# A written order for the head of a macaron block: FFN weight, four norms and five FFNs

## The chip, the core and the metric

The kernel runs on one core of one Trainium2 chip. The metric is the device time of one execution in microseconds (us), the median of several. Five engines matter: TensorE (PE: matmuls and transposes, with its weight loads as PEld), VectorE (DVE), ScalarE (ACT), GpSimd (POOL), and SyncE (SP), which here only issues DMAs. Each engine works through its own queue in order and waits on semaphores for the others.

## The reference: what is computed

The input is x of 4 x 4096 rows with 512 channels. One block is applied:

```
x = x + 0.5 * ffn(layernorm(x))
x = x + attention(layernorm(x))      # 16 heads of 32, 13 neighbours of each row, relative bias
x = x + 0.5 * ffn(layernorm(x))      # the same weight
```

The FFN is one 512 x 512 product with a bias. Before it, both operands are quantised: each run of 32 values in a row of the activations and of the weight is divided by its scale (its largest magnitude / 7.5), rounded to the nearest value of a 6-bit grid, ties to the lower one, and multiplied by the scale again. The attention has a product for queries, keys and values (1536 x 512, with bias) and an output product (512 x 512, with bias).

## The kernel before: stages, slots and the names that matter

**Tiles.** The 16384 rows are 128 tiles of 128 rows (`t`); four tiles make a group. Every large product is made in f16 parts: each operand is a high half and a low half, and `product` (L146 to L155) makes 12 matmuls of 128x128 by 128x512 (three pairs of halves, four chunks of channels). All weights lie in `wt`, channels first, in columns `QO, KO, VO, PO, FO` for queries, keys, values, output product and FFN.

**Stages of a tile.** `load`; `moments` (mean and variance on DVE); `quantised_norms`: POOL makes the factors, ACT the normed rows `yq`, DVE the block scales `sc` and `r`, POOL multiplies (L246), ACT rounds to fp8, POOL multiplies back (L251), ACT and DVE make the two halves `hlq`, and a transposing DMA makes `xT`. Then `ffn` (PE into `pmf`, DVE adds into x, L279), `first_half` (the attention's norm, halves `hln`, transposing DMA into `x2`), `values` (PE into `pmv`, halves `vt`, to DRAM), `project_qk`, `softmax`, `attend` and `project_out` by items of a group and a quarter of the channels, and `second_half` (the second FFN).

**The order of the work.** `begin(slot, stage, rank)` puts a stage (a Python generator) into a slot; `run_slot` runs what lies in a slot by rank, and each `yield n, rank` moves the rest n slots on. A tile comes every `STEP` = 7 slots: its first FFN at slot 7t+5, its values at 7t+20, the first query and key product at slot 38 (`QK`). From `manual_schedule()` on, the program order is the order of each engine's queue; before that call, a planner with its own times reorders the instructions.

**The head.** Inside the `setup` pool and ahead of `manual_schedule()`, so ordered by the planner, stand: loads of the FFN weight `fw`, of three tiles of x and of the 16 chunks `rows` of the other weights; the sums of squares (ACT, `junk`), from which `powers` makes power-of-two scales `up` and `down`; the FFN weight's block scales (`w_abs`, `w_sc`, `w_hi`, `w_lo`, `w_r`, L730 to L743); its quantisation in four chunks (L757 to L774; the two products of `wu` at L760 and the one at L771 are POOL's); four transposing DMAs that put it into `wt` (`put_weights`); and the quantised norms of tiles 0 to 2. After `manual_schedule()`, `put_scaled` (L789, L791) scales and splits the 16 other chunks, in slots 2 to 36, each with a transposing DMA; `scales` (slot 0), `put_table` (slot 26) and `attention_bias` (slot 28, a product `pmb`) stand beside them.

Of the kernel before, what the change touches and what calls it, by code (L numbers as in the profile page):

```python
# [37 lines left out]
P = 128  # L38
# [26 lines left out]
def macaron_kernel(  # L65
# [70 lines left out]
    def tie_to_lower(t):  # L136

        nc.vector.scalar_tensor_tensor(t, t, BELOW_ONE, t, ALU.mult, ALU.min)
        ti = t.bitcast(I32)
        nc.vector.tensor_scalar(ti, ti, 1, None, ALU.bitwise_or)

# [74 lines left out]
    def quantised_norms(slot):  # L220

        tiles, mv = together.pop(slot)
        n = len(tiles)
        rs, nb = factors(slot, "q", mv[0], n)
# [21 lines left out]
        nc.gpsimd.tensor_tensor(yb, yb, bc(r, QB), ALU.mult)  # L246
# [4 lines left out]
        nc.gpsimd.tensor_tensor(  # L251
# [3 lines left out]
        if spare:  # L255
            hl = xp.tile([P, dim], F32, tag="x", name=f"hlq{slot}").bitcast(F16)
            hl = hl.rearrange("p (u s k) -> p u s k", u=1, s=2)
        else:
            hl = hlp.tile([P, 2, 2, dim], F16, tag="hlq", name=f"hlq{slot}")[:, :n]
# [11 lines left out]
    def ffn(t, which):  # L271

        xT = ys.pop(t)
        pm = ps_m.tile([P, dim], F32, tag="mm", name=f"pm{which}_{t}")
        product(
            pm, lambda s, c: xT[:, s, c, :], lambda s, c: wt[:, s, c, FO : FO + dim]
        )
        yield 1, 8
        nc.vector.scalar_tensor_tensor(xs[t], pm, cf, xs[t], ALU.mult, ALU.add)  # L279

    def first_half(t):

        yield from ffn(t, "f1")
        yield 1, 2
        mv = sm.tile([P, 1, 2], F32, tag="mvn2", name=f"mvn2_{t}")
        statistics(t, "n2", mv[:, 0, :])
        yield 1, 2
        rs, nb = factors(t, "n2", mv)
        yield 1, 2
        y = yp.tile([P, 1, dim], F32, tag="yn2", bufs=1, name=f"yn2_{t}")  # L290
        nc.scalar.activation(y[:, 0], xs[t], AF.Identity, bias=nb, scale=rs)
        hl = hlp.tile([P, 1, 2, dim], F16, tag="hln2", name=f"hln2_{t}")
# [274 lines left out]
    EARLY = 3  # L567
    STEP = 7

    F1, V, QK, SC, PV, OUT, F2 = 5, 2 * STEP + 6, 5 * STEP + 3, 6 * STEP, 8 * STEP + 3, 13 * STEP + 2, 12  # L570

# [32 lines left out]
    for t in range(NT):  # L604
        k = t * STEP
        begin(k - 18, one(load, t), 0)
        enlist(k - 10, t, "n1")
        if not 0 < t < EARLY:
            begin(k - 11, one(moments, k - 10, t, "n1"), 1)
        begin(k + F1, first_half(t))  # L610
        begin(k + V, values(t))
        begin(k + F1, one(add_bias, t, half_ffn_b), 8)
        at = out_slot(t)
        begin(at - 5, one(add_bias, t, after_b), 8)
        enlist(at + 2, t, "n3")
        begin(at, project_out(t, at + 2))
        begin(at + 6 if t < LAST else second_slot(t) - 2, one(add_bias, t, half_ffn_b), 8)
        begin(second_slot(t), second_half(t))
    for slot in together:
        if slot >= EARLY * STEP - 10:  # L620
            begin(slot, quantised_norms(slot), 1)
# [12 lines left out]
    with tc.tile_pool(name="setup", bufs=1) as sp, tc.tile_pool(name="scratch", bufs=2) as scr:  # L634
# [10 lines left out]


        rows = {}

        sq = sp.tile([P, 5 * KC], F32, name="sq")
        first = min(slots)  # L650
        for slot in range(first, first + EARLY * STEP, STEP):
            run_slot(slot)
        for _ in quantised_norms(-10):
            pass
        chunks = (8, 9, 10, 11, 12, 13, 14, 15, 0, 4, 1, 5, 2, 6, 3, 7)
        for o in chunks:
# [3 lines left out]
        for o in (*range(4 * KC, 5 * KC), *chunks):  # L660
            src = fw[:, o - 4 * KC, :] if o >= 4 * KC else rows[o]
            junk = scr.tile([P, dim], BF16, tag="junk", name=f"junk{o}")
            nc.scalar.activation(junk, src, AF.Square, accum_out=sq[:, o : o + 1])
        ptb = ps_m.tile([P, 512], F32, tag="mm", name="ptb")
        nc.tensor.transpose(ptb[:, : 3 * KC], b12, ident[: 3 * KC, : 3 * KC])
        bT = sp.tile([P, 3 * KC], F32, name="bT")
        nc.vector.tensor_copy(bT, ptb[:, : 3 * KC])
        b2 = sp.tile([P, 3 * KC], F32, name="b2")
        nc.vector.scalar_tensor_tensor(b2, bT, 2.0 ** -8, bT, ALU.mult, ALU.mult)
        nc.vector.tensor_tensor(sq[:, : 3 * KC], sq[:, : 3 * KC], b2, ALU.add)  # L670
        top5 = sp.tile([P, 5], F32, name="top5")
        up = sp.tile([P, 5], F32, name="up")
        down = sp.tile([P, 5], F32, name="down")

        def powers(lo, hi):
# [7 lines left out]
            nc.tensor.transpose(ptn[:w, :P], top5[:, lo:hi], ident)  # L683
            most = sp.tile([w, 1], F32, name=f"most{lo}")
            nc.vector.tensor_reduce(most, ptn[:w, :P], AX.X, ALU.max)
            diag = sp.tile([w, w], F32, name=f"diag{lo}")
            nc.vector.tensor_scalar(diag, ident[:w, :w], most, 2.0, ALU.mult, ALU.mult)
            ones_w = sp.tile([w, P], F32, name=f"ones{lo}")
            nc.gpsimd.memset(ones_w, 1.0)
            pb = ps_m.tile([P, 512], F32, tag="mm", name=f"pb{lo}")  # L690
            nc.tensor.matmul(pb[:, :w], ones_w, diag, start=True, stop=True)
            e = sp.tile([P, w], I32, name=f"e{lo}")
            nc.vector.tensor_copy(e.bitcast(F32), pb[:, :w])
            nc.vector.tensor_scalar(e, e, 23, None, ALU.logical_shift_right)
            nc.vector.tensor_scalar(e, e, 131, None, ALU.add)
            nc.vector.tensor_scalar(e, e, 1, None, ALU.logical_shift_right)
            nc.vector.tensor_scalar(e, e, 97, None, ALU.max)
            u, d = up[:, lo:hi].bitcast(I32), down[:, lo:hi].bitcast(I32)
            nc.vector.tensor_scalar(u, e, -1, 264, ALU.mult, ALU.add)
            nc.vector.tensor_scalar(u, u, 23, None, ALU.logical_shift_left)  # L700
            nc.vector.tensor_scalar(d, e, -10, None, ALU.add)
            nc.vector.tensor_scalar(d, d, 23, None, ALU.logical_shift_left)

        powers(4, 5)
        nc.vector.tensor_scalar(cf, down[:, 4:5], 0.5 / XS, None, ALU.mult)
        nc.gpsimd.tensor_scalar(half_ffn_b, half_ffn_b, 0.5, None, ALU.mult)
# [9 lines left out]
        def small(name):  # L716
            return sp.tile([P, KC * NB], F32, name=name)

        w_abs, w_sc, w_hi, w_lo, w_r = (
            small(s) for s in ("w_abs", "w_sc", "w_hi", "w_lo", "w_r")  # L720
        )

        def split_scale():
            nc.vector.tensor_scalar(
                w_hi.bitcast(I32), w_sc.bitcast(I32), -4096, None, ALU.bitwise_and
            )
            nc.vector.tensor_tensor(w_lo, w_sc, w_hi, ALU.subtract)

        for o in range(KC):
# [4 lines left out]
        nc.vector.tensor_scalar(w_sc, w_abs, 1.0 / Q_MAX, None, ALU.mult)  # L734
        split_scale()
        nc.vector.scalar_tensor_tensor(w_abs, w_hi, -Q_MAX, w_abs, ALU.mult, ALU.add)
        nc.vector.scalar_tensor_tensor(w_abs, w_lo, -Q_MAX, w_abs, ALU.mult, ALU.add)
        nc.vector.scalar_tensor_tensor(w_sc, w_abs, 1.0 / Q_MAX, w_sc, ALU.mult, ALU.add)
        nc.vector.tensor_scalar(w_sc, w_sc, Q_EPS, None, ALU.max)
        nc.vector.reciprocal(w_r, w_sc)  # L740
        split_scale()
        w_back = small("w_back")
        nc.vector.tensor_scalar(w_back, w_sc, up[:, 4:5], F8_SCALE, ALU.mult, ALU.mult)  # L743

        def large(name, o, dt=F32):
            return scr.tile(
                [P, NB, QB], dt, tag=name, bufs=3 if name == "wu_" else KC, name=f"{name}{o}"
            )

        for o in range(KC):  # L750
# [5 lines left out]
            qh, q0 = large("wqh_", o, F16), large("wq0_", o)  # L756
            nc.vector.tensor_tensor(qh, fwb, per(w_r), ALU.mult)  # L757
            for i, b in enumerate((w_hi, w_lo)):
                u = large("wu_", f"{o}_{i}")
                nc.gpsimd.tensor_tensor(u, qh, per(b), ALU.mult)  # L760
                nc.vector.tensor_tensor(fwb, fwb, u, ALU.subtract)  # L761
            nc.vector.tensor_tensor(q0, fwb, per(w_r), ALU.mult)
            nc.vector.tensor_tensor(q0, q0, qh, ALU.add)  # L763
            q0f = q0.rearrange("p n q -> p (n q)")
            tie_to_lower(q0f)
# [5 lines left out]
            nc.gpsimd.tensor_tensor(fwb, w8, per(w_back), ALU.mult)  # L771
            hl = scr.tile([P, 2, dim], F16, tag="whl", bufs=4, name=f"whlf{o}")
            nc.scalar.copy(hl[:, 0, :], fw[:, o, :])
            nc.vector.tensor_tensor(hl[:, 1, :], fw[:, o, :], hl[:, 0, :], ALU.subtract)  # L774
            put_weights(4 * KC + o, hl)

        for t in range(1, EARLY):
            moments(t * STEP - 10, t, "n1")
            for _ in quantised_norms(t * STEP - 10):
                pass  # L780

        ctx.enter_context(tc.manual_schedule())

        def put_scaled(o):
            s = up[:, o // KC : o // KC + 1]
            hl = scr.tile([P, 2, dim], F16, tag="whl", bufs=4, name=f"whl{o}")
            nc.scalar.activation(hl[:, 0, :], rows[o], AF.Copy, scale=s)  # L789
            yield 1, 9  # L790
            nc.vector.scalar_tensor_tensor(  # L791
# [132 lines left out]
```

## Time and profile before

| what | us |
|---|---|
| median of 3 runs (lowest, highest) | 2367.79 (2367.39, 2368.29) |
| the profiled execution's own time | 2366.79 |
| its span, first to last instruction | 2365.0 |
| PE busy, share of the span | 2273.6 (96%) |
| DVE busy | 2022.5 (86%) |
| POOL busy | 1987.6 (84%) |
| ACT busy | 1326.8 (56%) |
| first matmul of an FFN | 58.23 |
| first matmul of a query and key product | 105.73 |

The span is 1.8 us shorter than the execution's own time, and that execution is 1.0 us below the median. "Busy" is the time in which an engine has an instruction under way; a duration in the trace includes what an instruction waits for within the engine, so the same operation can show 0.6 us alone and 1.5 us beside another engine. Instructions on one engine overlap by a little: the start of the next one is a better price than a duration. A matmul group of one `product` is shown as x12.

### The profile page before, as it was taken

How to read it: one execution, taken by the hardware profiler on the slowest of the kernel's cores; microseconds unless marked ns; L12 is line 12 of the kernel's file. 1: busy time of each engine (PE TensorE's matmuls, PEld its weight loads, DVE VectorE, ACT ScalarE, POOL GpSimd, SP SyncE). 2: the span in 40 equal slices, each digit the busy share in tenths (PEclk: the TensorE clock that was granted, in tenths of full speed). 3: DMA queues.
4: the chain of work that ended last, by engine and by line, in shares of the span. 5: the costliest groups of instructions: out<-in, count | busy, mean ns of one | idle time of the engine just before them, and what ended most of it. 6: DMA issues, size and time to landing. Idle time of an engine off the chain costs nothing.

```text
span 2365.0 us, 82328 instructions
## 1 busy us (share of the span) xinstructions
PE 2273.6 (96%) x35539; PEld 1115.4 (47%) x35539; DVE 2022.5 (86%) x3588; ACT 1326.8 (56%) x2080; POOL 1987.6 (84%) x2012
## 2 busy tenths in 40 slices
PE   0799999999999999999999999999999999999988
PEld 0255444444444444444444444444444444444543
DVE  8799888888888888888888888888888888888785
ACT  4466556555555555555555565555555555555542
POOL 5588888888888888888888888888888888888886
PEclk9899999999999999999999999999999999999999
DMA  5789787787777777777777778777777778677763
GB/s 154 146 168 165 156 160 155 147 159 156 151 157 152 156 158 153 156 152 158 153 157 153 153 159 154 153 154 156 158 151 160 151 152 160 153 152 155 133 121 104
DMA packets 925701, 360.59 MB, mean 152 GB/s; under 512 B 718876, under 2 KB 889752, under 8 KB 925336
## 3 DMA queue, kind: packets, MB, share of 16 engines
q1 hardware_dynamic: 924992, 354.79, 73.3%
q8 instruction: 278, 4.55, 0.9%
q10 hardware_dynamic: 344, 0.53, 0.1%
q14 instruction: 87, 0.71, 0.1%
HBM read 110.15 MB, written 67.29 MB: 75 GB/s over the span
## 4 chain that ended last, share of the span: by engine, by line
PE 94%; DVE 3%; DMA 1%; POOL 1%; issue 1%; ACT 0%; SPq 0%; DVEq 0%; ACTq 0%; POOLq 0%
PE pmqk L151 28%; PE pmf L151 27%; PE pmo L151 14%; PE pmv L151 14%; PE ps L442 7%; PE pv L512 3%; DVE fw L761 0%; DMA xT<-hlq 0%; DMA fw<-in_L_ffn_weight_dram 0%; DVE stn L180 0%; DVE wq L763 0%; DVE hlq L204 0%; DVE wqh L757 0%; DMA rows<-in_L_attn_qkv_w_dram 0%; DVE whl L791 0%
## 5 line engine op out<-in xcount | busy, mean ns | idle before, releaser
L151 PE MATMUL pmf<-wt,xT 128*128 128x512 f16 x3048 | 703.5, 381 | 9.1 <-DMA xT<-hlq 9.1
L151 PE MATMUL pmqk<-x,wt 128*128 128x512 f16 x3072 | 705.7, 379 | 1.4 <-DVE vt L315 1.4
L151 PEld LDWEIGHTS <-xT 128*128 128x128 f16 x3048 | 299.1, 98 | 373.7 <-DMA xT<-hlq 11.5
L151 PEld LDWEIGHTS <-wt 128*128 128x128 f16 x3072 | 289.6, 98 | 336.6 <-issue 1.9
L151 PE MATMUL pmv<-wt,x 128*128 128x512 f16 x1536 | 355.0, 381 | 5.1 <-DVE mvn L181 5.1
L246 POOL TENSOR_TENSOR yq<-yq,r 128x1024 f32<-128x1024 f32 (+1 forms) x141 | 246.5, 1748 | 130.0 <-DVE r L244 130.0
L151 PE MATMUL pmo<-wt,ring 128*128 128x512 f16 x1536 | 354.8, 381 | 0.8 <-issue 0.8
L573 POOL TENSOR_TENSOR x<-x,half_ffn_b 128x512 f32<-128x512 f32 x256 | 327.4, 1279 | 0.1
L279 DVE SCALAR_TENSOR_TENSOR x<-pmf,coef,x 128x512 f32<-128x512 f32 x256 | 179.7, 702 | 156.4 <-PE pmf L151 155.9
L314 ACT CAST vt<-pmv 128x512 f16<-128x512 f32 x128 | 74.9, 585 | 388.9 <-PE pmv L151 388.9
L539 ACT ACTIVATE ring<-pv 128x510 f16<-128x510 f32 (+8 forms) x224 | 82.3, 414 | 368.4 <-PE pv L512 368.4
L180 DVE BATCH_NORM_STATS2 stn<-x 128x6 f32<-128x512 f32 x384 | 265.3, 691 | 8.9 <-DMA x<-in_L_attn_x_dram 0.2
L251 POOL TENSOR_TENSOR yq<-q,sc 128x1024 f32<-128x1024 fp8e4 (+1 forms) x141 | 246.7, 1749 | 0.0
L151 PEld LDWEIGHTS <-x 128*128 128x128 f16 x1536 | 150.8, 98 | 188.1 <-DMA x<-hln 5.6
L377 DVE SCALAR_TENSOR_TENSOR qk<-pmqk,qk_b,qk 128x512 f16<-128x512 f32 x256 | 190.5, 744 | 42.2 <-ACT qk L373 41.1
L151 PEld LDWEIGHTS <-ring 128*128 128x128 f16 x1536 | 140.7, 98 | 159.4 <-issue 3.3
L249 ACT ACTIVATE q<-yq,nudge 128x1024 fp8e4<-128x1024 f32 (+1 forms) x141 | 149.9, 1063 | 114.3 <-POOL yq L246 106.1
L485 POOL TENSOR_TENSOR sf<-sf,total 128x714 f32<-128x714 f32 (+2 forms) x128 | 178.6, 1395 | 34.5 <-ACT yq L233 19.1
L373 ACT ACTIVATE qk<-pmqk,qk_b 128x512 f16<-128x512 f32 x256 | 176.1, 688 | 52.1 <-PE pmqk L151 50.8
L186 POOL TENSOR_SCALAR rsq<-mv 128x2 f32<-128x2 f32 (+1 forms) x141 | 130.1, 923 | 89.3 <-DVE mv L181 86.6
L233 ACT ACTIVATE yq<-x,nbq,rsq 128x512 f32<-128x512 f32 x254 | 193.0, 804 | 18.0 <-POOL nbq L192 17.5
L492 POOL TENSOR_TENSOR p<-sf,p 128x714 f16<-128x714 f32 (+2 forms) x128 | 192.6, 1504 | 0.0
(145 smaller groups left out, 3459.7 us busy)
## 6 DMA issues: line engine op xcount, KB each, us to landing
vs<-vd SPq DMA_DIRECT2D x144, 357.0 KB
x<-in_L_attn_x_dram SPq DMA_DIRECT2D x128, 256.0 KB
vd<-vt SPq DMA_DIRECT2D x128, 256.0 KB
out_dram<-x SPq DMA_DIRECT2D x128, 256.0 KB
vs<-vd SPq DMA_DIRECT2D x24, 378.0 KB
vs<-vd SPq DMA_DIRECT2D x24, 315.0 KB
rows<-in_L_attn_qkv_w_dram SPq DMA_DIRECT2D x12, 256.0 KB
xT<-hlq SPq DMA_TRANSPOSE x141
```

Of the source, the lines that this page charges most:

```text
L151: nc.tensor.matmul(pm, lhs(a, c), rhs(b, c), start=(n == 0), stop=(n == 3 * KC - 1))
L180: nc.vector.bn_stats(st, xs[t])
L233: nc.scalar.activation(y[:, u], xs[t], AF.Identity, bias=nb[:, u : u + 1], scale=rs[:, u : u + 1])
L246: nc.gpsimd.tensor_tensor(yb, yb, bc(r, QB), ALU.mult)
L251: nc.gpsimd.tensor_tensor(yb, q8.rearrange("p u (n q) -> p (u n) q", q=QB), bc(sc, QB), ALU.mult)
L279: nc.vector.scalar_tensor_tensor(xs[t], pm, cf, xs[t], ALU.mult, ALU.add)
L373: nc.scalar.activation(t[:, s, 0, KN:], pms[s], AF.Identity, bias=bias)
L377: nc.vector.scalar_tensor_tensor(t[:, s, 1, KN:], pms[s], bias, t[:, s, 0, KN:], ALU.add, ALU.subtract)
L442: nc.tensor.matmul(ps[rows, u, :sides, w * KN : (w + 1) * KN], t[rows, 0, part, q0 : q0 + QR], t[rows, 1, :sides, k0 : k0 + KN], start=par ...
L485: nc.gpsimd.tensor_tensor(s, s, bc(total[:, :n], KN), ALU.mult)
L492: nc.gpsimd.tensor_tensor(p[:, :n, KN : 2 * KN], s, ph, ALU.subtract)
L573: nc.gpsimd.tensor_tensor(xs[t], xs[t], b, ALU.add)
```

## The change

All of the head is put under `manual_schedule()`, and its order is written out: generators for the small and the large steps are advanced one at a time by `run(generator, n)`, and `both(o, n)` takes one step each of the weight's chunks o and o+1 with a small step behind each.

- POOL's three products of each FFN weight chunk go to DVE. So do both products of the quantised norms of tiles 0 to 3 (`mult`).
- The FFN weight and the values' weight get their channels first by TensorE transposes into PSUM (16 and 16 of 128x128 f32), from which ACT and DVE write the halves into `wt`: 8 transposing DMAs fewer.
- The norms of tiles 0 to 3 are written between the weight's steps; tiles 4 and 5 follow. FFN 0 and 1 are begun with the first half of the output channels (`begin_ffn`), as soon as two chunks of the weight are there.
- The first five FFNs, the values' weight and the start of the values of tile 0 follow in the written order. The slot loop then starts at 23 instead of 0. FFN 5 stands at slot 31 (before: 40), values 1, 2 and 3 at 24, 27, 33 (before: 27, 34, 41).
- `put_scaled` is left with 12 chunks, at slots 23, 25, 33, 35 (queries and keys of the first two quarters), 42, 44, 49, 51 and, for the output product, 56, 60, 64, 67 (before: all 16 by slot 36). `attention_bias` goes from slot 28 to 70, `put_table` from 26 to 31.
- The loads of six tiles of x and of `rows` are issued at the head in one list; the bias of tiles 0 and 1 is added by DVE, the FFN bias is halved by ACT.

The core of the diff:

```diff
+        mult = nc.vector if slot in N1[:4] else nc.gpsimd
...
-        nc.gpsimd.tensor_tensor(yb, yb, bc(r, QB), ALU.mult)
+        mult.tensor_tensor(yb, yb, bc(r, QB), ALU.mult)
...
+    def begin_ffn(t):
+        xT, n = ys[t], dim // 2
+        pm = ps_m.tile([P, dim], F32, tag="mm", name=f"pmf1_{t}")
+        product(pm[:, :n], lambda s, c: xT[:, s, c, :], lambda s, c: wt[:, s, c, FO : FO + n])
+        begun[t] = pm, n
...
+    N1 = (-6, -5, -4, -3, -2, -1)
+    FIRST, VALUES = (5, 6, 11, 20, 23, 31), (18, 21, 27, 33)
+    SOON, AHEAD = len(FIRST), 5
...
+        ctx.enter_context(tc.manual_schedule())
+        def run(g, n=1):
+            for _ in range(n):
+                next(g, None)
...
+        def channels_first(pt, w):
+            for c in range(KC):
+                nc.tensor.transpose(pt[:, c, :], w[:, c * P : (c + 1) * P], ident)
+        def values_weight(o, pt):
+            channels_first(pt, rows[o])
+            yield
+            h, l = (wt[:, s, :, o * P : (o + 1) * P] for s in (0, 1))
+            s = up[:, o // KC : o // KC + 1]
+            nc.scalar.activation(h, pt, AF.Copy, scale=s)
+            yield
+            nc.vector.scalar_tensor_tensor(l, pt, s, h, ALU.mult, ALU.subtract)
+            yield
...
+            for b in (w_hi, w_lo):
+                nc.vector.tensor_tensor(u, qh, per(b), ALU.mult)
+                yield
                 nc.vector.tensor_tensor(fwb, fwb, u, ALU.subtract)
+                yield
...
-            nc.gpsimd.tensor_tensor(fwb, w8, per(w_back), ALU.mult)
-            hl = scr.tile([P, 2, dim], F16, tag="whl", bufs=4, name=f"whlf{o}")
...
+            nc.vector.tensor_tensor(fwb, w8, per(w_back), ALU.mult)
...
+            channels_first(pt, fw[:, o, :])
+            h, l = (wt[:, s, :, FO + o * P : FO + (o + 1) * P] for s in (0, 1))
+            nc.scalar.copy(h, pt)
+            yield
+            nc.vector.tensor_tensor(l, pt, h, ALU.subtract)
+            yield
...
+        def both(o, n=1):
+            for _ in range(n):
+                run(ready[o])
+                run(small_ones)
+                run(ready[o + 1])
+                run(small_ones)
...
+        both(2)
+        begin_ffn(0)
+        moments(n1_slot(2), 2, "n1")
+        run(norms[2])
+        run(norms[1])
+        squares(*chunks[11:14])
+        both(2)
+        run(norms[2])
+        run(norms[1])
+        begin_ffn(1)
...
+        small_ones = powers(0, 4)
+        run(small_ones)
+        moments(n1_slot(3), 3, "n1")
+        run(norms[3])
+        run(ready[2])
+        run(ready[3])
+        run(norms[3])
+        run(small_ones)
+        run(norms[2], 2)
...
+        both(2)
+        firsts = {t: first_half(t) for t in range(AHEAD)}
+        run(firsts[0])
+        run(firsts[1])
+        run(v_weight[11])
+        run(norms[2])
+        run(norms[3])
...
-        for slot, o in zip((2, 4, 5, 6, 10, 13, 16, 19, 21, 23, 25, 27, 29, 31, 33, 35), chunks):
+        begin(24, one(scales), 3)
+        begin(24, firsts[3], 4)
+        begin(24, first_values[1], 5)
+        begin(24, norms[5], 1)
+        begin(26, firsts[4], 1)
+        for slot, o in zip((23, 25, 33, 35, 42, 44, 49, 51, 56, 60, 64, 67), chunks[4:]):
             begin(slot, put_scaled(o), 9)
-        begin(28, attention_bias(), 9)
-        begin(26, one(put_table), 9)
-        slot = first
+        begin(70, attention_bias(), 9)
+        begin(31, one(put_table), 9)
+        slot = min(slots)
```

## The prediction, made before the changed kernel ran

> **What bounds the kernel now.** I read the page's engine and slice rows first, then a table of busy time by stretch, then the timeline of PE, then that of DVE and POOL in the head.
>
> ```profile
> PE 2273.6 (96%) x35539; PEld 1115.4 (47%) x35539; DVE 2022.5 (86%) x3588; ACT 1326.8 (56%) x2080; POOL 1987.6 (84%) x2012
> PE   0799999999999999999999999999999999999988
> ```
>
> PE is full from the fourth slice on. Its idle time lies in the first two slices and at the end. The change doesn't touch the end, so only the head can pay. The table by stretch (columns: PE, PEld, DVE, ACT, POOL busy; PE clock; DMA share; GB/s) says who holds the head up:
>
> ```profile
> 7.00:20.00 13.00, 1.04 (x4) 0.58 (x4) 12.25 (x36) 9.96 (x29) 7.83 (x13) 1.00 0.98 356
> 20.00:35.00 15.00, 0.00 (x0) 0.00 (x0) 15.00 (x22) 4.25 (x13) 12.17 (x10) 1.00 0.24 72
> 35.00:47.00 12.00, 0.93 (x3) 0.58 (x3) 12.00 (x23) 4.85 (x8) 5.29 (x3) 1.00 0.26 50
> 47.00:58.20 11.20, 0.00 (x0) 0.00 (x1) 9.28 (x23) 5.78 (x9) 4.39 (x4) 1.00 0.52 100
> 72.90:82.50 9.60, 5.31 (x13) 1.67 (x13) 7.12 (x12) 5.82 (x10) 6.23 (x9) 0.68 0.67 137
> 94.00:105.70 11.70, 8.92 (x32) 3.48 (x32) 10.94 (x20) 6.63 (x11) 7.08 (x11) 0.78 0.88 168
> 105.70:117.30 11.60, 11.57 (x176) 5.72 (x176) 7.20 (x14) 5.63 (x9) 7.39 (x11) 1.00 0.64 139
> 128.90:140.50 11.60, 11.60 (x191) 5.72 (x177) 10.94 (x24) 7.62 (x13) 9.93 (x13) 1.00 1.06 210
> 140.50:152.80 12.30, 12.30 (x256) 6.21 (x243) 11.40 (x25) 7.86 (x14) 10.11 (x13) 1.00 0.88 161
> ```
>
> Until 58 us DVE is the bound; from 58 to 105.7 nobody is full: PE waits for chains through DVE, POOL, ACT and a DMA; from 105.7 PE is. Note the last two rows: there DVE has only 0.7 to 0.9 us idle in seven slots. PE's timeline shows what is done by then:
>
> ```profile
> 58.23 4.41 PE L151 MATMUL pmf<-wt,xT-10_160 128*128 128x512 f16 x12 [15.20 <-DMA wt<-whlf]
> 62.47 2.75 PE L151 MATMUL pmf<-wt,xT-3_391 128*128 128x512 f16 x12
> 82.49 4.24 PE L151 MATMUL pmf<-wt,xT 128*128 128x512 f16 x12 [4.27 <-DMA xT<-hlq]
> 105.73 5.34 PE L151 MATMUL pmqk<-x,wt 128*128 128x512 f16 x24 [1.40 <-DVE vt L315]
> ```
>
> By 105.73 PE has made five FFNs, three value products and `pmb`: nine, at 2.6 us from start to start when warm, 23 us of 106.
>
> **DVE and POOL in the head.** Price of a 128x512 step on DVE:
>
> ```profile
> 24.65 0.62 DVE L761 TENSOR_TENSOR fw<-fw,wu 128x512 f32<-128x512 f32 x1
> 26.64 1.53 DVE L761 TENSOR_TENSOR fw<-fw,wu 128x512 f32<-128x512 f32 x1
> 29.05 1.49 POOL L760 TENSOR_TENSOR wu<-wqh,w_hi 128x512 f32<-128x512 f16 x1
> 48.12 1.02 DVE L696 TENSOR_SCALAR e<-e 128x4 int32<-128x4 int32 x1
> ```
>
> The same step starts the next after 0.60 us alone and 1.46 us beside a POOL product; even a step of four elements took 1.02. Going through DVE's timeline from 14.9 to 52.1 us, some 20 instructions are stretched, by 15.5 us in all (start-to-start minus 0.60, or minus 0.12 for a small one). The change puts 20 products of POOL's on DVE in this stretch (12 of the weight, 8 of norms): 20 x 0.60 = 12.0. Here a rule speaks against it: the Trainium skill, "Perfetto Trace Analysis", section "Optimizing Scalar/DVE Operations", says that when DVE is saturated, moving work off to Scalar or even GpSimd may make sense, though the shared read port may spoil it. DVE is saturated here, so by the offloading half this move loses 12.0 us; by the rows it wins 15.5 - 12.0 = 3.5. I take the rows, since they show both cases of the same instruction.
>
> **Stage 1, to the complete FFN weight.** From 7.1 (second chunk landed) DVE has in the written order: three maxima 1.8; four chunks of ten steps at 0.60 and one at 0.36, 25.4; norms 0 and 1 whole at 3.7 (statistics 0.82, scales 1.09, two products, low half), 7.4; norm 2 without its low half 3.1; norm 3 up to its first product 2.5; some 50 small steps at 0.12, 6.1. Sum 46.3, so 53.4. Waits that I see: `powers(0, 4)` has its transpose on PE behind the begun FFN 1, which waits for `xT` of tile 1. The price of that way is the row at 77.43, where a low half ending at 79.19 let PE start at 82.49: 3.3 us, then 12 cold half-width matmuls of about 2.2 and a transpose of 0.37; DVE stands 3 us for it, with norms 2 and 3 and both last weight chunks queued behind. About 1.5 for the last PE transposes (four at the 0.37 of `ptn`, then ACT 0.6) and the hops of `powers(4, 5)`. So 58: no earlier than the 58.2 of now. The eight DMAs saved (3.3 us from issue to landing) lie in this sum as shorter hops. At the bounds: no waits 54, each doubled 62.
>
> **Stage 2, to the end of the written list.** Now only FFNs and halves are left, since norms 0 to 3 are made. DVE: four `first_half` additions with statistics at 1.48 (5.9), four values' weights at 0.66 (2.6), two bias additions (1.2), norm 4's scales (1.1), eight products and low halves at 0.60 (4.8), two statistics at 0.82 (1.6), small ones 0.6: 17.9. Beside it POOL makes four products (norm 4, two biases); each stretches at most one step by 0.86, so 0 to 3.4, I take 2.0; and about 1.3 for `vt` behind a cold value product. 58 + 21.2 = 79.2.
>
> **Stage 3, slots 24 to 38.** Up to norm 5's low half at slot 29 DVE has its scales 1.1, `scales` 0.8, two scaled chunks 1.3, two `vt` 1.2, an addition with statistics 1.5, two low halves 1.2: 7.1, and 8.1 beside POOL's two products: 87.3. Its DMA 3.3: 90.6. PE has by then idled about 4 us, and the row at 82.49 shows what 4.27 idle costs: 4.1 instead of 2.6. FFN 5 ends at 94.7, values 3 at 97.3, and the query and key product starts there instead of at 105.7: 8.4 us won, with ten products done in place of nine.
>
> **What that is worth later.** Slots 38 to 44 lose FFN 5 and values 3 and hold only the query product and the scores: 5.2 on PE, then ACT and DVE for its second half (in before they end 6.9 after its start), scores 1.2, some slack: 8.6 instead of 11.6, 3.0 more won. `pmb` comes back at slot 73: 2.6 lost. In slots 42 to 74 DVE gets eight chunks and two bias steps at 0.67 or more. Two of them fit in the thin stretch; for the other eight there is idle time of 0.7 to 0.9 per seven slots, some 4.4 over six stretches. All of it filled, they cost 8 x 0.67 - 4.4 = 1.0; none filled and each beside POOL, 8 x 1.46 = 11.7. The scaled steps now (L791) are mostly 0.73 to 0.75 long with a few of 1.2, so I take 2.5. ACT's 0.72 for each hides in its four idle us. The eight DMAs with them meet a DMA share of 0.9 to 1.06; cover is the slack of the attention's transposes (seven slots, 12 us); without it, up to one 3.3 us landing. I cost them at nothing.
>
> Sum: 8.4 + 3.0 - 2.6 - 2.5 = 6.3. Against the profiled execution's own 2366.8 that is 2360.5; its median is 1.0 above it, so 2361.5.
>
> **Rivals.**
> - *Packed*: DVE never stands and POOL doesn't disturb. Stage 1 ends at 54.4, stage 2 after 17.9 at 72.3, norm 5 at 79.4, the query product at 89.4. Then 16.3 + 3.0 - 2.6 - 1.0 = 15.7: 2352. For it: the head's 20 products leave POOL nearly empty. Against: the visible waits.
> - *A queue written too tight*: a fixed order can't dodge; if DVE's standing in the head sums to 12 instead of 6, the query product starts at 103.5, and 2.2 + 3.0 - 2.6 - 2.5 leaves 0.1: 2367.7. That the change then doesn't do what it says is this case.
> - *Slower*: DVE in slots 42 to 74. It has under 1 us free in seven slots; ten added steps, each with two SBUF inputs, each beside a POOL that is 80% busy, at 1.46 make 14.6, and PE waits for its queries and PSUM behind them. It turns the sign from 8.8 us; at 14.6 the kernel takes 2366.8 + 5.8 + 1.0 = 2373.6.
>
> **Numbers.** This kernel's measurement can tell about 0.2%, 4.7 us, from no change: 2363.1 to 2372.5. My forecast 0.50 (itself 2357 to 2365, so 0.44 faster, 0.06 same), packed 0.25, too tight 0.13, slower 0.12 (0.01 of it inside the bound). Faster 0.69, same 0.20, slower 0.11. The range leaves out the slower case and a rest of the packed one: 2351 to 2368.
>
> **What would show it.** `wt` complete near 58 and DVE above 90% busy to there; 128x512 steps at 0.6 to 0.7 long before 55 us; FFNs 0 to 3 within 10 us; the first `pmqk` near 97; one gap of DVE behind `ptn` near 47; L791's steps and small PE gaps between 117 and 175; from 190 on the same pace as now. It is wrong if the weight is complete far from 58, if PE idles more than 5 us after its first `pmqk`, or if stretches beyond 200 us change.

## The result, and the profile after

The change made the kernel slower: a median of 2393.97 us (four runs, 2390.65 to 2397.55) against 2368.04, a ratio of 1.011 with a 95% interval of 1.0092 to 1.0127. The prediction's best single figure was 2361.5 and its range 2351 to 2368. The profiled execution took 2391.95, 25.2 more than that of before. The first two lines of the page that answer to those of before, engines and slices:

```profile
PE 2288.8 (96%) x35595; PEld 1126.0 (47%) x35595; DVE 2018.2 (84%) x3621; ACT 1326.6 (56%) x2081; POOL 1963.6 (82%) x1989
PE   2689999999999999999999999999999999999988
```

PE starts earlier, and the digits hide the rest: the loss lies within slices that still say 9. The table by stretch (columns: PE, PEld, DVE, ACT, POOL busy; PE clock; DMA share; GB/s):

```profile
20.00:35.00 15.00, 1.97 (x8) 1.57 (x8) 14.73 (x41) 6.59 (x15) 2.50 (x3) 1.00 0.75 246
47.00:58.20 11.20, 6.18 (x31) 4.09 (x30) 9.90 (x31) 5.72 (x9) 1.08 (x3) 0.65 0.02 4
94.00:105.70 11.70, 10.15 (x38) 4.20 (x39) 3.77 (x9) 2.63 (x4) 0.75 (x2) 0.75 0.31 72
105.70:117.30 11.60, 5.42 (x143) 3.20 (x142) 7.06 (x18) 5.15 (x8) 7.71 (x10) 0.84 0.73 121
140.50:152.80 12.30, 8.43 (x215) 4.25 (x214) 11.20 (x22) 7.92 (x13) 9.10 (x12) 0.79 1.04 171
```

In the first row 41 DVE instructions stand where 22 stood before: DVE is as full, but no longer stretched. From 94 to 105.7 DVE, ACT and POOL have nearly nothing to do, and from 105.7 to 117.3, where PE was full before, it is half idle. In the last row PE lacks 3.9 us of its 12.3. "Cold" below is a product of 12 matmuls that takes 4 to 5 us instead of 2.76 behind a wait; the clock granted to PE is 0.75 to 0.84 in the stretches where this happens. PE's timeline names the waits:

```profile
56.11 2.72 PE L141 MATMUL pmf<-wt,xT-6_396 128*128 128x256 f16 x12 [2.46 <-DVE wt L886]
95.55 4.91 PE L141 MATMUL pmf<-wt,xT-1_834 128*128 128x512 f16 x12 [9.00 <-DMA xT-1_834<-hlq-1_828]
102.89 5.34 PE L141 MATMUL pmqk<-x,wt 128*128 128x512 f16 x24
114.40 1.87 PE L457 MATMUL ps<-qk 32*32 32x84 f16 x128 [6.17 <-DVE qk L392]
116.20 7.41 PE L141 MATMUL pmqk<-x,wt 128*128 128x512 f16 x24
...
149.19 0.66 PE L527 MATMUL pv<-pT,vs 126*32 126x30 f16 x60 [3.06 <-DMA vs<-vd]
149.77 5.10 PE L141 MATMUL pmqk<-x,wt 128*128 128x512 f16 x12
...
180.83 0.63 PE L527 MATMUL pv<-pT,vs 126*32 126x30 f16 x60 [2.78 <-DMA vs<-vd]
181.81 4.44 PE L141 MATMUL pmb<-wt,vbx 128*128 128x512 f16 x12 [0.36 <-issue]
```

Start of the query and key products in both traces, after minus before: first 102.89 (2.8 us ahead), second 116.20 (1.1 ahead), fourth 142.40 (1.8 behind), fifth 161.13 (8.3 behind), seventh 195.17 (17.6 behind), ninth 222.73 (17.7 behind). The ninth, in after and in before:

```profile
222.73 2.75 PE L141 MATMUL pmqk<-x,wt 128*128 128x512 f16 x12
205.01 2.75 PE L151 MATMUL pmqk<-x,wt 128*128 128x512 f16 x12
```

So 18.7 us are lost between 116 and 195, and another 7.5 between 223 and the end, where the two kernels do the same work. The late loss shows as small gaps that wait for nothing. In the timeline of PE beyond 200 us, before has three of them (1.7 us in all), after has twelve (10.2). Some near the end:

```profile
2262.07 1.68 PE L141 MATMUL pmo<-wt,ring 128*128 128x512 f16 x7 [0.78 <-issue]
2275.22 2.55 PE L141 MATMUL pmo<-wt,ring 128*128 128x512 f16 x11 [1.37 <-issue]
...
2316.05 1.46 PE L141 MATMUL pmf<-wt,xT 128*128 128x512 f16 x6 [0.94 <-issue]
```

A group of 12 is split there into 5 and 7, 1 and 11, 6 and 6: PE stops in the middle of one product, and the trace shows nothing that releases it ("issue"). Counting the matmuls between the first two gives 7+12+68+12+12+144+1 = 256. With as many weight loads that is 512 instructions. The part of the page on DMA queues says what this may be (queue, packets, MB, share; kernel before):

```profile
q8 instruction: 278, 4.55, 0.9%
```

4.55 MB in 278 packets is 16.4 KB each. PE has some 71,000 instructions; at the 64 bytes that the Trainium skill gives an instruction ("Perfetto Trace Analysis", "The 4-stage abstract model") they are by this estimate 4.55 MB, the whole of this queue. One packet is then 256 instructions, and the gaps lie two packets apart. The Trainium skill, "Runtime: NRT & Kernel Launch", "Terms", says that an engine's instruction memory is refilled in blocks of 16 KiB, which agrees with the packets.

The trace's records of single packets tie the two together. The PE timelines of all 18 traces have 120 gaps put down to issue; 118 of them end 1.2 to 1.6 us after a packet of q8 has landed, though such a packet comes only every 7 to 8 us (median distance). So what PE waits for in these gaps is its next block of instructions.

### The profile page after: what moved, and what is told of

It reads as the page before. It is cut to its first block, busy times and chain, and to the rows that moved or that the text cites. A ratio compares the mean times of both kernels' runs of the same rounds, so it can differ in the third digit from the quotient of the medians.

```text
span 2390.2 us, 82388 instructions
## 1 busy us (share of the span) xinstructions
PE 2288.8 (96%) x35595; PEld 1126.0 (47%) x35595; DVE 2018.2 (84%) x3621; ACT 1326.6 (56%) x2081; POOL 1963.6 (82%) x1989
## 3 DMA queue, kind: packets, MB, share of 16 engines
q8 instruction: 278, 4.55, 0.8%
## 4 chain that ended last, share of the span: by engine, by line
PE 92%; DVE 4%; DMA 1%; POOL 1%; issue 1%; ACT 1%; SPq 0%; DVEq 0%; POOLq 0%; ACTq 0%
PE pmqk L141 28%; PE pmf L141 27%; PE pmo L141 14%; PE pmv L141 14%; PE ps L457 6%; PE pv L527 3%; DMA vs<-vd 1%; DVE stn L170 0%; DVE qk L392 0%; DVE x L283 0%; DMA fw<-in_L_ffn_weight_dram 0%; DVE wu L856 0%; DVE fw L858 0%; DVE hlq L194 0%; POOL yq L243 0%
## 5 line engine op out<-in xcount | busy, mean ns | idle before, releaser
L141 PE MATMUL pmf<-wt,xT 128*128 128x512 f16 x3000 | 690.0, 380 | 5.0 <-DMA xT<-hlq 4.0
L141 PEld LDWEIGHTS <-xT 128*128 128x128 f16 x3000 | 293.5, 98 | 361.7 <-DMA xT<-hlq 6.4
```

The lines of the kernel that those rows point to most:

```text
L141: nc.tensor.matmul(pm, lhs(a, c), rhs(b, c), start=(n == 0), stop=(n == 3 * KC - 1))
```

## The experiments

Four causes were told apart: the waits at FFN 5 (theory B in the expectations); the late weights' transposes in SP's queue, ahead of the loads of `vs` (L and Q); the place at which PE's instructions are refilled (R); and the tiles' addresses (S). The change puts `up`, `down` and `vb` into the constants' pool, so every later tile lies 96 bytes higher. All ratios are against the kernel before (medians of 2367.8 to 2368.2 beside these runs).

**Addresses.** A tile of 96 bytes that nothing uses, in the kernel before; then 32 more bytes in the changed kernel, 128 in all:

```diff
+    pad = const.tile([P, 24], F32, name="pad")      # before + 96 bytes
+    pad = const.tile([P, 8], F32, name="pad")       # after + 32 bytes
```

> The kernel before, with one unused tile of 96 bytes put behind the constants, so that every later tile in SBUF lies 96 bytes further on, at odd multiples of 32 bytes, as in the changed kernel; the work and its order are the same. Theory S (the shift of addresses makes every DMA to and from SBUF slower, and with it the loads of the stacks and of instructions): slower than before by 5 to 12 us, mean DMA share up from 0.75 to about 0.79 between 500 and 2000 us, and some 5 to 10 short gaps of PE in the middle of a matmul group that are put down to issue. Rival (the 25 us come from the late weights and the head alone): within 1 us of before, DMA share 0.75.

Measured: 2371.42, ratio 1.0015 (1.0007 to 1.0022), 3.6 more and less than the 5 to 12 expected.

> The changed kernel with a further unused 32 bytes behind the constants, so that the tiles lie at multiples of 64 bytes again. Theory S: 8 to 15 us faster than the changed kernel's 2394, so 2379 to 2386, DMA share back to 0.75 in the steady part, the gaps put down to issue gone, and less waiting for the stacks near 146 and 178 us. Rival: 2391 to 2397, nothing else changed.

Measured: 2383.40, ratio 1.0068 (1.0056 to 1.0081): 10.6 less than after. And the kernel before with 128 bytes:

> The kernel before with an unused tile of 128 bytes behind the constants, so that the later tiles lie as in the realigned kernels; nothing else. It is the base for the late weights and tells whether the lower DMA share there (0.69 to 0.70 instead of 0.75) comes from the addresses alone. Address theory: DMA share 0.69 to 0.70, time within 2 us of before (PE is the bound, 2366 to 2368), so that the late weights alone cost 6 to 8 us. Rival (share comes from the changed order): DMA share 0.75.

Measured: 2367.44, ratio 0.9996 (0.9987 to 1.0004). The rows of the table by stretch from 500 to 900 us (last two columns: DMA share, GB/s) are these for before as it is:

```profile
500.00:900.00 400.00, 399.41 (x6241) 196.49 (x6240) 347.16 (x611) 228.19 (x352) 345.77 (x340) 1.00 0.75 155
```

Before with 96 bytes:

```profile
500.00:900.00 400.00, 399.19 (x6291) 196.43 (x6278) 346.28 (x611) 229.23 (x354) 345.81 (x341) 1.00 0.79 155
```

Before with 128 bytes:

```profile
500.00:900.00 400.00, 399.87 (x6242) 196.84 (x6240) 347.49 (x612) 228.30 (x352) 346.09 (x340) 1.00 0.70 156
```

The same bytes keep the DMA engines busy for 0.75, 0.79 or 0.70 of the time. The kernel before loses 3.6 us or nothing by it; the changed kernel, whose share in this stretch falls from 0.78 to 0.69 when it is realigned, wins 10.6. Of these, 6.2 are gone by the ninth query product (216.56 instead of 222.73), where PE waits less for `vs` (1.67 near 176 instead of 2.78 near 181) and runs the products behind its waits less cold; the other 4.4 are what the gaps put down to issue shrink by (10.2 to 5.8, see the table below). Which of the moved tiles does it isn't settled.

**Late weights.** In the realigned kernel all scaled chunks go back ahead of slot 37:

```diff
-        for slot, o in zip((23, 25, 33, 35, 42, 44, 49, 51, 56, 60, 64, 67), chunks[4:]):
+        for slot, o in zip((23, 25, 26, 27, 28, 29, 31, 32, 33, 34, 35, 36), chunks[4:]):
```

> The realigned changed kernel with the eight late weight chunks scaled and transposed in slots 26 to 36 instead of 42 to 67. Theory L (the late chunks' transposing DMAs stand in the one DMA queue ahead of the stack loads, and their DVE steps fill a full DVE): PE doesn't wait for the stacks at the first and third item, and it takes 6 to 10 us less than the realigned kernel, unless the head grows by as much. Rival (DMA rate alone, theory S): no more than 2 us from the realigned kernel.

Measured: 2378.61, ratio 1.005 (1.0036 to 1.0063), 4.8 less than without this edit, and no wait for `vs` from 138 to 190. The gain is below the 6 to 10 expected because the head grows: the second query product starts at 119.55 instead of 116.37. The other way round, the kernel before (128 bytes) with its chunks in the order and late slots of the change, and the bias at 70:

> The kernel before, its tiles at multiples of 64 bytes, with only one part of the change: the order of the chunks and the late slots of the changed kernel (42 to 67 for eight chunks, bias at 70). Theory L: PE waits 3 to 8 us for the stacks or the scores after 140 us, and what the head wins by six chunks fewer (2 to 6 us) is lost again: 2366 to 2374. Rival (the late chunks hide): faster than before by 4 to 8 us.

Measured: 2374.35, ratio 1.0028 (1.0017 to 1.0039), 6.9 above the same without, although its first query product starts 5.4 earlier (100.25 against 105.68). It has PE wait 0.55 and 2.65 us for `vs` at 142 to 145 and 1.98 at 173.86. The timeline of SP's queue (start, duration of the issue) shows how, first in after:

```profile
138.73 1.26 SPq L749 DMA_TRANSPOSE wt<-whl  x1
...
142.82 1.76 SPq L433 DMA_DIRECT2D vs<-vd  x2
```

The same load in before:

```profile
137.43 1.07 SPq L418 DMA_DIRECT2D vs<-vd  x2
```

Issuing one transpose holds SP for 1.23 us or more. The load of the second part of `vs` stands behind a late weight's, behind those of `xT` and `hln` and, ahead of these, that of `pT` with 2.93 us; the load starts at 142.82 instead of 137.43, though PE is only 1.8 us late there. In the realigned kernel, loading it three slots after the first part instead of seven:

```diff
-                yield STEP, 9
+                yield 3, 9
```

> The realigned changed kernel with its late weights, and only the last part of each stack load (the low half of the values) issued 3 slots after the first part instead of 7, ahead of the late weights' DMAs of those slots. Theory Q (the stack arrives late because its issue stands in the DMA queue behind the late weights' transposes): PE's waits for the stack near 144 to 148 and 176 are gone or under 1 us, 4 to 8 us faster than 2383.4. Rival (the DMA engines are full, or VectorE is late): waits of the same size, at the stack or at the next transfer, within 2 us.

Measured: 2380.55, ratio 1.0052 (1.0038 to 1.0066): 2.9 less, under the 4 to 8 expected. The waits for `vs` near 145 and 176 are gone, but at 176.29 PE now waits 4.13 for `hln`. That row, and the ninth query product in this run and in the realigned kernel without the edit:

```profile
176.29 5.16 PE L143 MATMUL pmb<-wt,vbx 128*128 128x512 f16 x12 [4.13 <-DVE hln L196]
217.80 2.75 PE L143 MATMUL pmqk<-x,wt 128*128 128x512 f16 x12
216.56 2.75 PE L143 MATMUL pmqk<-x,wt 128*128 128x512 f16 x12
```

So the place in SP's queue is the cause of those waits, but taking them away wins nothing by here: the run is even 1.2 us behind, since other waits of their size stood behind them. The 2.9 come later. The edit moves the loads of every group and puts 44 more semaphore instructions into PE's own queue (142 instead of 98 in the traces), which moves the refills too; the gaps beyond 200 us are 3.2 us instead of 5.8.

**FFN 5.** In the realigned kernel, with late weights and then with early ones:

```diff
-    FIRST, VALUES = (5, 6, 11, 20, 23, 31), (18, 21, 27, 33)
+    FIRST, VALUES = (5, 6, 11, 20, 23, 40), (18, 21, 27, 41)
```

> The same one edit on the realigned kernel with its late weights (2383.4). Theory B: the first query product at 88 to 93, time 2374 to 2378. Rival: 2381 to 2385.

Measured: 2376.03, ratio 1.0036 (1.0024 to 1.0048), 7.4 less. The first query product stands at 90.57, the second at 106.30, 11.0 ahead of before; by the ninth (208.96) it is 4.0 behind.

> The realigned changed kernel with the weights early, and FFN 5 put back to slot 40 and the values of tile 3 to slot 41, where the kernel before has them; nothing else of the head changes. Theory B (FFN 5 in slot 31 waits in PE's queue for xT of tile 5, values 3 and the query product wait behind it, and VectorE, ScalarE and POOL wait in turn for values 3 with the next norms behind): PE's idle of 10 us near 98 is gone, the first query product starts at 90 to 95, and the time is 6 to 10 us under that with early weights alone (2378.6), so 2369 to 2373. Rival (the slots are held up by the engines' load, not by that wait): the next wait takes its place, the first query product starts before 98 but the second one still at 117 to 120, and the time stays within 2 us.

Measured: 2373.40, ratio 1.0021 (1.0015 to 1.0028), 5.2 less than with early weights alone.

**The place of refilling.** The kernel before has PE's queue moved on by small matmuls at its start, while PE idles; nothing reads what they write:

```diff
+        for _ in range(56):        # 112 instructions; in the control 256, two whole blocks
+            nc.tensor.matmul(
+                pt_v[:32, 1, :30], spare_in[: 3 * KN, :32], spare_in[: 3 * KN, :30], start=True, stop=True
+            )
```

> The kernel before with 128 spare bytes (2367.4), and 56 such small matmuls (112 instructions) at PE's start, so that the later PE instructions lie where they lie in the changed kernel, modulo 512. Theory R: gaps put down to issue appear among the last output products (two to four, 0.5 to 2.5 us each) and the kernel takes 2 to 6 us more: 2369 to 2373. Rival: no such gaps, 2366 to 2369.

Measured: 2380.24, ratio 1.0052 (1.0039 to 1.0064): 12.8 above the same without. The control:

> The kernel before with the 128 byte tile and 256 small matmuls that nothing reads at the start of TensorE's queue: 512 instructions more, a whole distance between two of the gaps put down to fetching, so that every later instruction lies at the same place as before. Theory R (it is the place at which TensorE's queue is refilled that costs): as without them, 2366 to 2370, and no issue gap above 1 us behind 2200. Rival (the spare matmuls or their tile themselves cost, so that the 12.8 us of the run with 56 of them say nothing of the place): 2378 or more, since there are more of them.

Measured: 2366.66, ratio 0.9995 (0.9987 to 1.0003). So the place costs, not the matmuls. PE's timeline of the run with 56, near the end:

```profile
2237.64 1.28 PE L444 MATMUL ps<-qk 32*32 32x84 f16 x136
2238.85 0.60 PE L153 MATMUL pmo<-wt,ring 128*128 128x512 f16 x2
2242.57 3.93 PE L153 MATMUL pmo<-wt,ring 128*128 128x512 f16 x10 [3.12 <-issue]
...
2297.64 1.35 PE L444 MATMUL ps<-qk 32*32 32x84 f16 x144
2298.93 1.04 PE L153 MATMUL pmf<-wt,xT 128*128 128x512 f16 x4
2304.10 3.46 PE L153 MATMUL pmf<-wt,xT 128*128 128x512 f16 x8 [4.14 <-issue]
```

Each gap lies within or just behind a group of scores: 144 small matmuls, 288 instructions in 1.35 us, more than a block. In the trace a block's packet is under way for 1.1 us (median), and PE goes on 1.2 to 1.6 us after it has landed, together more than the 1.2 us that 256 such instructions last. In the two largest gaps here the packet even began only after PE had stopped: at 2239.90 in the gap from 2239.45 on, and at 2301.49 in that from 2299.96 on. In the kernel before a packet begins, by an estimate from the places of the gaps, with some 220 instructions still to go (median; at most about 300): PE fetches about one block ahead. All gaps of this kind beyond 200 us, in one profiled execution of each:

| kernel | tiles moved by | matmuls ahead of the loop, against before | gaps, us | median time |
|---|---|---|---|---|
| before | 0 bytes | 0 | 3, 1.7 | 2368.0 |
| before, shifted | 96 | 0 | 5, 3.6 | 2371.4 |
| before, shifted | 128 | 0 | 2, 0.9 | 2367.4 |
| before, 56 spare | 128 | 56 | 7, 12.3 | 2380.2 |
| before, 256 spare | 128 | 256 | 2, 1.1 | 2366.7 |
| after | 96 | 56 | 12, 10.2 | 2394.0 |
| after, realigned | 128 | 56 | 7, 5.8 | 2383.4 |

The first three have one and the same PE queue, so their gaps differ by the addresses alone, and they follow the DMA shares 0.75, 0.79 and 0.70. The changed kernel has 56 matmuls more than before in the trace, the same 112 instructions. With 200 spare ones the later work comes back to its old places:

> The changed kernel as it is (addresses too) with 200 spare matmuls ahead, which bring the instructions of the later stretches back to the places that they have in the kernel before, modulo 512. Theory R with the size that the gaps show (about 9 us of issue gaps, 7.5 of them gone with it): 2384 to 2388, gaps behind 2200 gone. Rival (the gaps only fill time that another wait takes, or come at other places): 2391 or more.

Measured: 2386.21, ratio 1.0085 (1.0072 to 1.0098): 7.8 less than after. Its ninth query product starts at 224.06, 19.1 behind before, and it ends 18.7 behind: nothing is lost after 224 any more. Its gaps beyond 200 us are 4.6 us instead of 10.2.

> The realigned kernel with the weights early and FFN 5 back in slot 40 (2373.4), with 200 small matmuls into a spare PSUM corner at PE's start, which nothing reads. They bring the place of every later PE instruction back to where it is in the kernel before, modulo 512 instructions (the changed kernel's PE stream is some 110 longer). Theory R (PE stalls where a block of its instructions has to be fetched; the gaps put down to issue lie 256 matmuls, 512 instructions, apart, and it hangs on the place whether they hide): the gaps near 2242, 2255 and 2298 us and those at 141 and 155 are gone, and 3 to 6 us with them: 2367 to 2370. Rival (the gaps come from contention of DMAs whatever the place): as many gaps, 2372 to 2376.

Measured (the version with early weights and FFN 5 back, plus 200 spare): 2370.64, ratio 1.0009 (1.0 to 1.0017). The gaps at 141, 155 and behind 2240 are gone, a new one of 3.08 us is at 204.84.

**A better version.** From that with FFN 5 back and late weights: chunks spread out to slot 78, the bias at 80, the second part of `vs` three slots after the first, 200 spare matmuls:

```diff
+        for slot, o in zip((23, 25, 33, 35, 40, 43, 46, 51, 57, 64, 71, 78), chunks[4:]):
+        begin(80, attention_bias(), 9)
+                yield 3, 9
```

> All that the runs point to, on the realigned changed kernel with FFN 5 back in slot 40 (2376.0): the late weights spread to one chunk in seven slots (queries and keys at 40, 43, 46, 51, output product at 57, 64, 71, 78, the bias at 80), the low part of the stack loads 3 slots after the first, and the 200 spare matmuls. If queue, VectorE's filling and refill are the three causes behind the head: PE's waits for the stack and for query halves between 100 and 180 us go from 11 us to under 3, and the time is 2359 to 2364, faster than both kernels. If the head's gain is lost to something else: 2367 or more.

Measured: 2379.36, ratio 1.0048 (1.0036 to 1.0061), a miss by 15. The spare matmuls were to put its refills at the instructions of before, yet it has gaps of 1 to 3 us (1198, 1731 and others). Without the spare matmuls:

> The version with FFN 5 and values 3 back, the stack loaded earlier and the late weights spread, without the 200 spare matmuls that it had. Theory R for its miss (its TensorE order put the refills at bad places): another time than 2379.4 by several us, 2362 to 2372 if the places are kind, with other gaps than at 172.81, 203.37, 1198 and 1731. Rival (its spread loads and transposes slow it wherever the refills lie): 2377 to 2382 again.

Measured: 2373.75, ratio 1.0026 (1.0015 to 1.0037), the gaps elsewhere. Then the loads of `vs` moved for the first group alone, with and without spare matmuls:

```diff
+                yield 3 if (b, g) == (0, 0) else STEP, 9
```

> The spread version with 200 spare matmuls (2379.4), but the second parts of the stacks are loaded earlier for the first group only; the later groups load them seven slots after the first parts, as in the kernel before. Places of refilling and late transfers are then those of before. If a refill costs by what the DMA queues carry just then: the gaps of the run at 594, 1198, 1518 and 1731 go, 2366 to 2371. If the place alone decides: 2377 to 2381 again.

Measured: 2371.52, ratio 1.0012 (1.0005 to 1.0019); only small gaps are left (2.0 us in all).

> The same without the spare matmuls, so with the places of refilling 112 instructions later (2373.8 with all stacks loaded earlier). If the place alone decides: 2372 to 2376 again. If place and transfers decide together, as the bad run of before with 56 spare matmuls suggests: gaps behind 2200 as there, 2374 to 2384.

Measured: 2377.26, ratio 1.0037 (1.0023 to 1.0051), with the gaps of the run with 56 back near the end, at or next to the same groups: 2.44 us in a `pmo` at 2245.22, 1.86 and 0.98 at 2260 and 2275, 3.83 in a `pmf` at 2303.90.

With all loads moved, the spare matmuls cost 5.6 (2379 against 2374); with the loads of before, they win 5.7 (2372 against 2377). It is tempting to say that the same places cost or not by what the DMA queues carry just then, but these four runs don't show it: the runs with all loads moved have the 44 more semaphore instructions in PE's queue, so their refills drift away from the places of before. Near 1946 the gap stands in a `pmqk` there (first line), in a `pmo` in the kernel before:

```profile
1945.96 1.04 PE L143 MATMUL pmqk<-x,wt 128*128 128x512 f16 x4 [1.54 <-issue]
1946.84 1.24 PE L151 MATMUL pmo<-wt,ring 128*128 128x512 f16 x5 [0.80 <-issue]
```

That the DMA side matters is shown by the three address runs of the table alone. No version beats the kernel before.

## Why the prediction was wrong, point by point

In the prediction's own terms: the 8.4 won up to the first query product were 2.8; the 3.0 of slots 38 to 44 became 1.7 lost; the 2.6 and 2.5 lost in the later slots became 18.7 lost up to the seventh query product (195); and behind it, where nothing was to change, 0.2 up to the ninth and 7.5 to the end were lost. Together, but for rounding, these are the 25.2.

- *Stage 1, the weight complete at 58.* Right, and reached 2 us sooner: the last half of `wt` (L886) starts at 55.37, the second half of FFN 0 at 56.11. DVE's 128x512 steps run at 0.60 (a pair, 1.20 from start to start), as the rows said against the offloading half of the rule that is cited there.
- *Stage 2, the written list ends at 79.2.* The number is right: DVE's last step of the list, the low half of tile 2's `hln` at 78.77, is over at 79.4. This is in part luck, since the stage took 23.4 instead of 21.2 and began 2 us early; DVE stood 1.78 for ACT and 1.85 and 1.22 for POOL's bias additions. FFNs 0 to 3 end within 10 us, as told (the first halves of 0 and 1 were made before).
- *Stage 3, first query product at 97.3.* The term was mis-sized by 5.6 us: 102.89. From the end of the list norm 5's low half took 12.9 instead of 8.1 and ends near 92.3 instead of 87.3: `scales` took 2.07 instead of 0.8, and DVE stood twice for a `vt` of ACT:

```profile
84.61 0.69 DVE L330 TENSOR_TENSOR vt<-pmv,vt 128x512 f16<-128x512 f32 x1 [1.33 <-ACT vt L329]
91.09 0.69 DVE L330 TENSOR_TENSOR vt<-pmv,vt 128x512 f16<-128x512 f32 x1 [2.95 <-ACT vt L329]
```

  Its DMA took the 3.3 that was counted (PE goes on at 95.55), and FFN 5, after 9.0 of waiting instead of the 4 counted, ran cold for 4.9. The longer stand comes through ACT and POOL: ACT's `vt` lies behind the half of norm 5, which waits for POOL. POOL's second product of this norm had its operand at 85.8 but stands in POOL's queue behind the factors of the next `first_half`, which wait for DVE. POOL's timeline:

```profile
86.99 0.54 POOL L176 TENSOR_SCALAR rsn<-mvn 128x1 f32<-128x1 f32 x1 [4.53 <-DVE mvn L171]
...
88.88 1.04 POOL L243 TENSOR_TENSOR yq-1_752<-q_-1_808,sc-1_761 128x512 f32<-128x512 fp8e4 x1
```

- *Slots 38 to 44 in 8.6 us.* Mis-sized by 4.7: 13.3. The prediction took FFN 5 and values 3 out of these slots and forgot what they hold up just ahead. ACT and DVE have the halves of values 3 in front of the halves of the queries, and wait for PE:

```profile
103.08 0.58 ACT L329 CAST vt<-pmv 128x512 f16<-128x512 f32 x1 [6.77 <-PE pmv L141]
```

  The rest follows in their order: DVE's `vt` at 103.70, POOL's factors at 106.08, the query halves at 112.95, the scores at 114.40 after 6.17 us idle. Putting FFN 5 and values 3 back gave 7.4 and 5.2 us.
- *The eight DMAs with the late chunks, "I cost them at nothing".* Failed. The cover named, the slack of the attention's transposes, was the wrong one: behind them in SP's queue stand the loads of `vs`, with no slack. The bound given, one landing of 3.3, was too low as well, since it came twice, near 149 and 181, with a smaller wait ahead of it each time, and left PE cold. From the second query product to 195 the timeline shows 3.8 + 3.8 us of waits in front of `pv` (1.1 of it for `hln`), then 2.3 + 1.8 of products at 5.10 and 4.44 instead of 2.76 and 2.6, 2.1 of the second query product at 7.41 instead of 5.34, which the 6.17 of waiting ahead of it had left cold, and `pmb` itself, 2.6 as predicted. These are 16.4 of the 18.7; 11.7 of them are the waits in front of `pv` and the cold products behind them. In the realigned kernel the same take 7.4; early weights remove them but hold up the head by 3.2, which leaves 4.8. Alone, late weights cost 6.9 in the kernel before; with FFN 5 and values 3 back, early weights win 2.6.
- *The added DVE steps in slots 42 to 74, 2.5 us, and the slower rival built on them.* Not borne out: where PE waits from 120 to 190, DVE ends waits of 0.5 us at most. The rival had the sign by the wrong engine.
- *"From 190 on the same pace as now".* This is the step that failed outright, and "The change doesn't touch the end" with it. 7.5 us are lost behind 223. The 56 more matmuls of the head move every later refill of PE's queue; with 200 more, which bring the places back, nothing is lost there (7.8 less in all). The prediction's own test ("if stretches beyond 200 us change") tells it.
- *A term that the prediction does not have: the addresses.* `up`, `down` and `vb` in the constants' pool move all later tiles by 96 bytes, which was put at nothing without a reason. Realigning wins 10.6, in part by shortening the waits and gaps of the points above.

The four causes don't add up one by one, since a wait that goes uncovers another. One path through the runs gives the sizes: 2394.0 after, 2383.4 realigned, 2376.0 with FFN 5 and values 3 back, 2373.4 with the weights early too, 2370.6 with the refills back, 2368.0 before. Of the last 2.6, the one new gap at 204.84 is 3.1. What the written head wins is given back by the ninth query product in each of the seven versions with FFN 5 back: it starts there at 204.7 to 209.0, before at 205.01. In the spread one without spare matmuls the second product is 10.0 us ahead of before, the fifth 4.2 (between them PE waits 1.9 us for DVE's query halves and 2.9 for a transposing DMA of `hln`), the eighth 0.4 (`pmb`, 2.6, and a gap of 0.7), the ninth 0.3. Which of the late steps makes those halves and `hln` late was not taken apart further.

## What to carry to other kernels

Work taken out of a head that is bound elsewhere has to land somewhere: list, for each moved step, every in-order queue that it enters and what stands behind it there, the DMA-issuing queue first. When PE is nearly full, read the gaps whose releaser is "issue" and see whether groups are split in the middle; if so, some hundred instructions more or less ahead of a long loop can cost or win some 10 us, and a control with a whole number of blocks tells this from the change itself. Moving a load can also change the number of semaphore instructions in PE's queue, and so these places. A tile added to an early pool moves all later ones, so pad an experiment to the same addresses before its parts are compared.

## What was unexpected in the hardware

- 112 PE instructions placed in idle time cost 12.8 us of 2367, and 512 cost nothing (ratio 0.9995). Of the 120 gaps of PE without a releaser, 118 end 1.2 to 1.6 us after the landing of a 16 KB packet of instructions.
- The same transfers take 0.70 to 0.79 of the DMA engines' time by a shift of all tiles of 96 or 128 bytes, at an unchanged 155 GB/s.
- After waits of 3.8 us, the next product of 12 matmuls took 5.10 and 4.44 us instead of 2.76 (after, 149.77 and 181.81), so that such a wait of PE cost half as much again; after 2.88 us of waiting (the spread version without spare matmuls, 148.66) it took 2.75.
